# Moving the spline's scale from its absolute values to its clamps, with a planner that no longer holds engines back for the scan

## The chip, the cores and the metric

The kernel runs on one NeuronCore of a Trainium2 chip, as one launch. The metric is the device time in microseconds of one execution; lower is better. Short names of the engines: PE is TensorE (matmuls; PEld its weight loads), DVE is VectorE, ACT is ScalarE, POOL is GpSimd, SP is SyncE, which issues the DMAs here.

## The reference

The input `x` has shape (32, 128, 56, 56): 32 images, 128 channels, 3136 pixels each. Four residual layers follow each other, each `x = x + f(gn(x))`, where `gn` is a group normalisation over 32 groups of four channels:

- layer 0, dynamic convolution: a 128x128 mixing matrix made from the pooled image, then a depthwise 3x3 filter at three dilations, each through SiLU;
- layer 1, spline: each value is clipped to [-2, 2] and put through a cubic B-spline with ten coefficients and 14 knots;
- layer 2, linear attention: pooled 8x8 queries and keys, values from a 128x128 matrix, a depthwise 3x3 filter;
- layer 3, a Mamba layer: layer norm, projection, a causal filter of four taps, and a state-space scan.

The two parts that matter here, cut down:

```python
knots = jnp.linspace(GRID_MIN, GRID_MAX, NUM_KNOTS)      # -2, 2, 14
xc = jnp.clip(x, GRID_MIN, GRID_MAX)                     # x is group-normalised
basis = _bspline_basis(xc, knots)                        # cubic
return jnp.einsum('...n,n->...', basis, coeffs)
...
def step(h, inp):
    dA_t, dBu_t, C_t = inp
    h = dA_t * h + dBu_t                                 # 256 channels x 16 states
    y = jnp.einsum('bdn,bn->bd', h, C_t)
```

## The kernel before

**Tiles.** An image lives in SBUF as a tile of 128 channels by 3136 pixels (`xt`), worked on in seven chunks of 448 pixels. Three images are in flight: one in the scan, the next in layers 1 and 2, the one after that in layer 0. The hardware loop runs five times over six images; two images follow it, and a prologue prepares the first ones.

**The scan.** A chunk has 16 steps (`STEPS`), 112 per image. In each step:

- ACT makes the decays, two tiles `da <- delta,alog` of 128x448 in PSUM (`decay`). There are two such buffers in all, so a `da` waits until the scan of the step before has read its buffer.
- PE spreads the rows of B into `pb` once every two steps (`b_rows`, a single PSUM buffer), and of C into an `mm` tile, which ACT copies to `cb` (`c_rows`, two steps ahead).
- DVE multiplies `h <- du,pb` (128x896) and runs two scans `h <- da,last,h` (`state`). `h` has three buffers.
- ACT copies the last column to `last`, POOL multiplies `hc <- h,cb` (`products`; two buffers), and PE adds `hc` over the states into `y <- hc,sums` (`add`).

At a chunk's end DVE multiplies `sz` by `y`, PE applies `outT`, DVE adds to `xt`, and SP stores.

**The spline** (`spline`, from line 747). With u the normalised value in units of the knots' distance, it needs relu(1 - |u - m|) for the twelve inner knots m; linear combinations of these, two of them cubed, give the spline. For a chunk of 448 pixels SP copies 32 channels four times below each other (`stack <- xt`), so that four knots stand in one tile; three knot sets times four channel blocks make twelve `Abs` on ACT (128x448, line 801), and after every three a `Relu` over all three (128x1344, the clamp, line 803). A column operand of 128x1 gives each partition its own number: before, `Abs` takes both a scale `scl` and a bias `bia`, and the clamp only a bias `one`. `scl` and `bia` are made once per image: statistics (`group_stats`) give the mean `mg`, the variance with its epsilon `ve`, and `rs` = ve to the power -1/2; two columns `ab` are spread over the partitions by 16 small matmuls with `ident` into `pab`; DVE adds the knots' numbers `kneg` (line 517). `top` is the place above which the last basis function's end value is added.

**The order of the work.** All instructions outside the setup go through a planner (`Plan`). The calls only record pieces of work, each with its engine, the tiles it reads and writes, a price (`price`, line 163) and a step of the scan at which it stands. The planner derives due times backward through the dependencies, then goes forward in time (`attempt`, line 245): for each engine it picks among the pieces whose inputs are done, takes the one that can begin first over all engines, and so fixes the order in which each engine's in-order queue is written. Work of the scan and of the inputs of the next chunk is marked with `ahead > 0`; layers 0, 1 and 2 are filler with `ahead == 0`. Among one engine's pieces the choice is by

```python
late = at - self.PATIENCE[e] * (w.ahead > 0)
...
key = (max(late, free[e]), w.due, i)
```

Here `at` is when a piece can begin, and `free[e]` when its engine becomes free. A piece of the scan that will only be ready within `PATIENCE[e]` us of that is treated like one that is ready, and by its due time it usually goes first, with the engine idle until then. The planner's price for an activation adds 0.09 us for each column operand:

```python
columns = sum(isinstance(kw.get(k), bass.AP) for k in ("bias", "scale"))
w.cost += 0.06 + 8.34e-4 * n + 0.09 * columns + 0.03 * (args[1].space != bass.MemoryType.PSUM)
```

Since the planner's queues are issued from one place, nearly every instruction in the profile has the line of that place (L338); groups are told apart by the tiles' names.

Of the kernel before, what the change touches and what calls it, by code (L numbers as in the profile page):

```python
# [12 lines left out]
F32 = mybir.dt.float32  # L13
F32R = mybir.dt.float32r
AF = mybir.ActivationFunctionType
ALU = mybir.AluOpType
AX = mybir.AxisListType

P = 128
# [3 lines left out]
CH = ROWS * W  # L23
# [8 lines left out]
G = 32  # L32
NG = P // G
# [9 lines left out]
NKNOT = 14  # L43
GMIN, GMAX = -2.0, 2.0
# [49 lines left out]
class Plan:  # L94
# [7 lines left out]
    TABLE = 1.28  # L102
    NEVER = 1e18
    GATE, BUSY = 3.413, 1.27
    PATIENCE = {"tensor": 0.5, "scalar": 0.5, "gpsimd": 0.3, "vector": 0.1, "sync": 0.0}

    def __init__(self, nc, tc):
        self.nc, self.tc = nc, tc
# [136 lines left out]
    def attempt(self, born, behind):  # L245
# [6 lines left out]
        left = dict(self.uses)  # L252
        free = {e: 0.0 for e in self.PATIENCE}
        ready = {e: [] for e in self.PATIENCE}
        slots, held, table, bus, first, loads = {}, {}, None, 0.0, 0, {}
# [8 lines left out]
        while len(out) < len(works):  # L264
# [4 lines left out]
            for e, cand in ready.items():  # L269
                for i in cand:  # L270
# [6 lines left out]
                    if at >= self.NEVER:  # L277
                        continue
                    late = at - self.PATIENCE[e] * (w.ahead > 0)
                    if w.table and w.table != table:  # L280
# [82 lines left out]
def tile_conv_stack(ctx: ExitStack, tc: tile.TileContext, out: bass.AP, x: bass.AP, w: dict):  # L363
    nc = tc.nc
# [4 lines left out]
    def pool(name, bufs, **kw):  # L369
        return Rotation(plan, ctx.enter_context(tc.tile_pool(name=name, bufs=bufs, **kw)), name, bufs)  # L370

    const = ctx.enter_context(tc.tile_pool(name="const", bufs=1))
    small = pool("small", 2)
# [67 lines left out]
    def column(name, value):  # L441
        t = const.tile([P, 1], F32, name=name)
        nc.vector.memset(t[:], value)
        return t

    mhalf = column("mhalf", -0.5)
    one = column("one", 1.0)
# [62 lines left out]
    kneg = const.tile([P, len(KNOTS)], F32, name="kneg")  # L510
# [3 lines left out]
    for s, knots in enumerate(KNOTS):  # L514
        for k, m in enumerate(knots):
            rows = slice(G * k, G * k + G)
            nc.vector.memset(kneg[rows, s : s + 1], -float(m))
            for i, (f, s1) in enumerate(SUMS):
                if s1 == s and (f == 2 or m % 2 == f):
                    nc.vector.tensor_copy(cs[rows, i : i + 1], (qc if f == 2 else py_)[rows, m - 1 : m])  # L520
# [59 lines left out]
    nc = plan  # L580

    def psum(cols=CH, rows=P):
        t = ps_mm.tile([P, 512], F32, tag="mm", name="mm")
        return t[:rows, :cols]
# [15 lines left out]
    def group_stats(st):  # L600

        mv = small.tile([P, 2], F32, tag="mv", name="mv")
        nc.vector.bn_aggr(mv[:], st[:].rearrange("p a b -> p (a b)"))
        pm = psum(1)
        nc.tensor.matmul(pm, gmat[:], mv[:, 0:1], start=True, stop=True)
        mg = small.tile([P, 1], F32, tag="mg", name="mg")
        nc.vector.tensor_copy(mg[:], pm)
        dm = small.tile([P, 1], F32, tag="dm", name="dm")
        nc.vector.tensor_sub(dm[:], mv[:, 0:1], mg[:])
        vv = small.tile([P, 1], F32, tag="vv", name="vv")  # L610
        nc.vector.scalar_tensor_tensor(vv[:], dm[:], dm[:, 0:1], mv[:, 1:2], ALU.mult, ALU.add)
        pv = psum(1)
        nc.tensor.matmul(pv, gmat[:], vv[:], start=True, stop=True)
        ve = small.tile([P, 1], F32, tag="ve", name="ve")
        nc.vector.tensor_scalar_add(ve[:], pv, GN_EPS)
        rs = small.tile([P, 1], F32, tag="rs", name="rs")
        nc.gpsimd.tensor_tensor(rs[:], ve[:], mhalf[:], ALU.pow)
        return mg, rs, ve, dm
# [127 lines left out]

    def spline(xt, st):
        mg, rs, ve, _ = group_stats(st)
        ab = small.tile([P, 2], F32, tag="ab", name="ab")

        kpu = (NKNOT - 1) / (GMAX - GMIN)
        nc.vector.tensor_scalar_mul(ab[:, 0:1], rs[:], kpu)
        nc.vector.tensor_mul(ab[:, 1:2], mg[:], ab[:, 0:1])
        nc.vector.tensor_scalar(ab[:, 1:2], ab[:, 1:2], -1.0, -GMIN * kpu, ALU.mult, ALU.add)

        top = small.tile([P, 1], F32, tag="top", name="top")
        nc.vector.tensor_mul(top[:], ve[:], rs[:])
        nc.scalar.activation(top[:], top[:], AF.Identity, bias=mg[:, 0:1], scale=GMAX)
        pab = psum(2 * NG)
        for c in range(NG):  # L760
            for k in range(4):
                nc.tensor.matmul(
                    pab[G * k : G * k + G, 2 * c : 2 * c + 2],
                    ident[:, G * c : G * c + G],
                    ab[:],
                    start=True,
                    stop=True,
                    tile_position=(0, G * k),
                )
        pab = pab.rearrange("p (c t) -> p c t", t=2)  # L770
        scl = small.tile([P, NG], F32, tag="scl", name="scl")
        nc.vector.tensor_copy(scl[:].unsqueeze(2), pab[:, :, 0:1])
        bia = small.tile([P, NG, 3], F32, tag="bia", name="bia")
        nc.vector.tensor_add(
            bia[:], kneg[:].unsqueeze(1).to_broadcast([P, NG, 3]), pab[:, :, 1:2].to_broadcast([P, NG, 3])
        )

        def load_u(j):

            t = stk.tile([P, NG, ROWS * PW], F32, tag="stack", name="stack")  # L780
            with plan.together():
                for k in range(4):
                    for c in range(NG):
                        nc.sync.dma_start(
                            t[G * k : G * k + G, c, 0:CH], xt[G * c : G * c + G, j * CH : (j + 1) * CH]
                        )
            return t

        us = [load_u(0)]
        after = Stats(xt)  # L790
        yield 6.0
        for j in range(NCH):
            if j + 1 < NCH:
                us.append(load_u(j + 1))
            u = us[j]
            xs = xt[:, j * CH : (j + 1) * CH]
            hats = wide.tile([P, NG, 3, CH], F32, tag="wide", name="hats")
            for c in range(NG):
                for s in range(3):
                    nc.scalar.activation(  # L800
                        hats[:, c, s, :], u[:, c, 0:CH], AF.Abs, bias=bia[:, c, s : s + 1], scale=scl[:, c : c + 1]
                    )
                nc.scalar.activation(hats[:, c], hats[:, c], AF.Relu, bias=one[:, 0:1], scale=-1.0)
                yield 3.6
            ind = tmp.tile([P, CH], F32, tag="v", name="ind")
            nc.gpsimd.tensor_scalar(ind[:], xs, top[:, 0:1], clast, ALU.is_ge, ALU.mult)

            def combined(f):
                ps = psum()
                mine = [i for i, (f1, _) in enumerate(SUMS) if f1 == f]  # L810
                for i in mine:
                    with plan.together(NG):
                        for c in range(NG):
                            nc.tensor.matmul(
                                ps[G * c : G * c + G, :],
                                wspl[:, i, :],
                                hats[:, c, SUMS[i][1], :],
                                start=(i == mine[0]),
                                stop=(i == mine[-1]),
                                tile_position=(0, G * c),  # L820
                            )
                return ps

            ps = combined(2)
            nc.vector.tensor_add(xs, xs, ps)
            nc.gpsimd.tensor_add(xs, xs, ind[:])
            after.take(j)
            yield 2.2
            for f in range(2):
                ps = combined(f)  # L830
                sq = tmp.tile([P, CH], F32, tag="v", name="sq")
                nc.scalar.activation(sq[:], ps, AF.Square)
                cube = tmp.tile([P, CH], F32, tag="v", name="cube")
                nc.vector.tensor_mul(cube[:], sq[:], ps)
                nc.gpsimd.tensor_add(xs, xs, cube[:])
                yield 1.7
        after.take(NCH)
        return after.st
# [307 lines left out]
    def until_scan(b):  # L1146

        xt = xts[b % 3]
        st = yield from spline(xt, sts[b % 2])
        st = yield from linear_attention(xt, st)  # L1150
        norm = carried[b % 2]
        norm_weights(st, *norm)
        yield 5.0
        layer_norm(xt, xns[b * NCH % 3], 0, norm)
        yield 5.0
# [233 lines left out]
```

## Time and profile before

| what | us | from |
|---|---|---|
| median of three runs | 16343.33 (16294.26 to 16363.43) | the times |
| the profiled execution | 16316.11 | the times |
| its span in the profile | 16314.3 | the page |
| the scans `h<-da,last,h` and `h<-da,h` | 6772.7 + 1054.1, 7168 of them | groups of instructions |
| the products `h<-du,pb` | 3788.6, 3584 of them | groups of instructions |
| `hats<-stack,bia,scl` (the Abs) | 1887.6, 2688 of them at 754 ns | groups of instructions |
| `hats<-hats,one` (the clamps) | 1261.5, 896 of them at 1408 ns | groups of instructions |
| table loads of ACT | 656.9, 512 of them | groups of instructions |

A group's row gives the engine, the operation, the tiles written and read with their shapes, the count, the busy time and the mean duration of one, and then the time that the engine stood idle just before these instructions with what ended it. A row of the list of waits has the waiter, the one that released it, the total, the number of waits and the longest one. The busy times of engines overlap, so they don't add up to the span. PEclk is the granted clock of PE in tenths of full speed; it was 0.893 in the mean.

### The profile page before, as it was taken

Reading aid. Unit: us, or ns where it says so; the run is one execution under the profiler, and the core shown is the slowest. Engines: PE = TensorE matmul, PEld = TensorE weight load, DVE = VectorE, ACT = ScalarE, POOL = GpSimd, SP = SyncE. Lnnn points to the kernel's source line nnn. Section 1 sums busy time; section 2 is a strip of 40 time slices with the busy share of each in tenths; the row PEclk is TensorE's granted clock in tenths of the full one; section 3 lists DMA queues with packets and bytes.
Section 4 is the critical chain, followed back from the end, with each engine's and each line's share of the span. In section 5 each row is a group of like instructions: output and inputs, shape, how many; then the busy total and the mean of one; then the engine's idle time right before and its main releaser. Section 6 shows DMA issues by size and latency. Waiting matters only on the chain. (4 is left out here: it accounts for less than half of the span.)

```text
span 16314.3 us, 212520 instructions
## 1 busy us (share of the span) xinstructions
PE 14202.3 (87%) x66400; PEld 4559.9 (28%) x66400; DVE 14306.2 (88%) x17314; ACT 11713.4 (72%) x21127; POOL 10785.0 (66%) x6406
## 2 busy tenths in 40 slices
PE   6888898888898888988888888888888898888887
PEld 2222222222222222222222222222222222222222
DVE  2898988989889898899988888888898898888889
ACT  3777777777677776777776777767777677776675
POOL 2676666666666666667666666666676666766666
PEclk7888998889998898998989988899988899888888
DMA  6344444344443444434444434444344444344421
GB/s 143 93 101 98 98 112 96 89 99 101 106 104 88 100 97 101 109 94 94 101 99 107 102 86 98 99 105 107 91 98 97 100 108 106 85 97 99 101 56 34
DMA packets 986159, 1589.93 MB, mean 97 GB/s; under 512 B 175622, under 2 KB 611209, under 8 KB 984331
## 3 DMA queue, kind: packets, MB, share of 16 engines
q1 hardware_dynamic: 985002, 1576.06, 41.0%
q8 instruction: 538, 8.81, 0.2%
q14 instruction: 619, 5.06, 0.1%
HBM read 785.62 MB, written 173.18 MB: 59 GB/s over the span
## 5 line engine op out<-in xcount | busy, mean ns | idle before, releaser
L338 POOL TENSOR_TENSOR hc<-h,cb 128x896 f32<-128x896 f32 x3584 | 7476.1, 2092 | 4173.5 <-DVE h L338 2178.7
L338 DVE TENSOR_TENSOR_SCAN h<-da,last,h 128x448 f32<-128x448 f32 x6144 | 6772.7, 1135 | 498.2 <-ACT da L338 451.3
L338 ACT ACTIVATE da<-delta,alog 128x448 f32<-128x448 f32 x7168 | 4481.8, 633 | 2635.3 <-DVE h L338 2369.4
L338 PE MATMUL y<-hc,sums 128*64 128x448 f32 x14336 | 3997.9, 638 | 625.6 <-POOL hc L338 617.8
L338 DVE TENSOR_TENSOR h<-du,pb 128x896 f32<-128x896 f32 x3584 | 3788.6, 1072 | 247.5 <-POOL hc L338 118.2
L338 PE MATMUL mm<-stack,dsT 96*32 96x448 f32 (+1 forms) x16128 | 1890.8, 575 | 59.4 <-DMA stack<-padded 16.8
L338 ACT ACTIVATE hats<-stack,bia,scl 128x448 f32<-128x448 f32 x2688 | 1887.6, 754 | 33.9 <-DVE bia L338 31.7
L338 PE MATMUL mm<-xn,winT 128*128 128x448 f32 x3584 | 1703.8, 590 | 39.8 <-ACT cb L338 13.5
L338 PEld LDWEIGHTS y<-hc,sums 128*64 128x64 f32 x14336 | 807.6, 147 | 2412.9 <-POOL hc L338 1436.9
L338 PE MATMUL mm<-hats,wspl 128*32 128x448 f32 x12544 | 1386.1, 563 | 33.3 <-ACT hats L338 30.4
L338 PE MATMUL pb<-dbl,sel 64*128 64x448 f32 x1792 | 918.3, 512 | 421.2 <-DVE h L338 364.3
L338 ACT ACTIVATE hats<-hats,one 128x1344 f32<-128x1344 f32 x896 | 1261.5, 1408 | 0.1
L338 ACT COPY cb<-mm 128x448 f32<-128x448 f32 x1792 | 940.3, 527 | 379.4 <-POOL hc L338 184.0
L338 PE MATMUL mm<-dbl,sel 64*128 64x448 f32 x1792 | 892.3, 502 | 363.5 <-DVE sz L338 63.7
L338 ACT ACTIVATE t<-mm 128x448 f32<-128x448 f32 x1568 | 829.2, 534 | 484.6 <-PE mm L338 480.3
L338 POOL TENSOR_TENSOR xt<-xt,g 128x448 f32<-128x448 f32 x672 | 767.5, 1142 | 524.1 <-DVE g L338 491.1
L338 DVE TENSOR_TENSOR_SCAN h<-da,h 128x448 f32<-128x448 f32 x1024 | 1054.1, 1070 | 28.3 <-ACT da L338 26.3
L338 PEld LDWEIGHTS mm<-xn,winT 128*128 128x128 f32 x3584 | 631.8, 197 | 986.0 <-issue 805.1
L338 DVE SCALAR_TENSOR_TENSOR g<-t,mm 128x448 f32<-128x448 f32 x672 | 407.7, 607 | 443.7 <-ACT t L338 392.8
L338 PEld LDWEIGHTS mm<-stack,dsT 96*32 96x32 f32 (+1 forms) x16128 | 445.2, 112 | 1156.3 <-issue 899.9
L338 PEld LDWEIGHTS mm<-dbl,sel 64*128 64x128 f32 x1792 | 351.2, 198 | 1453.5 <-issue 420.0
L338 PEld LDWEIGHTS pb<-dbl,sel 64*128 64x128 f32 x1792 | 358.6, 200 | 1419.1 <-issue 791.8
(187 smaller groups left out, 16166.2 us busy)
## 6 DMA issues: line engine op xcount, KB each, us to landing
stack<-padded SPq DMA_DIRECT2D x2688, 264.0 KB
stack<-xt SPq DMA_DIRECT2D x3584, 56.0 KB
delta<-delta SPq DMA_DIRECT2D x1792, 112.0 KB
du<-du SPq DMA_DIRECT2D x1792, 112.0 KB
padded<-yc SPq DMA_DIRECT2D x224, 264.0 KB
padded<-yc SPq DMA_DIRECT2D x256, 231.0 KB
xt<-x_dram SPq DMA_DIRECT2D x224, 224.0 KB
out_dram<-xt SPq DMA_DIRECT2D x224, 224.0 KB
```

Of the source, the lines that this page charges most:

```text
L338: call()
```

## The change

It has two parts. The spline's `Abs` no longer scales: it takes |x - mean - knot x deviation| on the raw value, and the clamp multiplies by -kpu x rs and adds one. For that, `kneg` holds the negated knot in the spline's own units, `ab` has three columns (the negated scale, the deviation ve x rs, the negated mean), and `bia` is made by a multiplication and an addition. A chunk has twelve instructions with a column operand less and four with one more. Second, all of `PATIENCE` becomes zero, so the planner takes what can begin first and looks at due times only among pieces that could begin at the moment the engine is free. Both parts change the planner's inputs, so the order of nearly all queues is made anew.

```diff
-    PATIENCE = {"tensor": 0.5, "scalar": 0.5, "gpsimd": 0.3, "vector": 0.1, "sync": 0.0}
+    PATIENCE = {"tensor": 0, "scalar": 0, "gpsimd": 0, "vector": 0, "sync": 0.0}
...
-            nc.vector.memset(kneg[rows, s : s + 1], -float(m))
+            nc.vector.memset(kneg[rows, s : s + 1], -GMIN - m * (GMAX - GMIN) / (NKNOT - 1))
...
-        ab = small.tile([P, 2], F32, tag="ab", name="ab")
+        ab = small.tile([P, 3], F32, tag="ab", name="ab")
         kpu = (NKNOT - 1) / (GMAX - GMIN)
-        nc.vector.tensor_scalar_mul(ab[:, 0:1], rs[:], kpu)
-        nc.vector.tensor_mul(ab[:, 1:2], mg[:], ab[:, 0:1])
-        nc.vector.tensor_scalar(ab[:, 1:2], ab[:, 1:2], -1.0, -GMIN * kpu, ALU.mult, ALU.add)
+        nc.vector.tensor_scalar_mul(ab[:, 0:1], rs[:], -kpu)
+        nc.vector.tensor_mul(ab[:, 1:2], ve[:], rs[:])
+        nc.vector.tensor_scalar_mul(ab[:, 2:3], mg[:], -1.0)
...
-        nc.vector.tensor_mul(top[:], ve[:], rs[:])
-        nc.scalar.activation(top[:], top[:], AF.Identity, bias=mg[:, 0:1], scale=GMAX)
-        pab = psum(2 * NG)
+        nc.scalar.activation(top[:], ab[:, 1:2], AF.Identity, bias=mg[:, 0:1], scale=GMAX)
+        pab = psum(3 * NG)
...
-        nc.vector.tensor_add(
+        nc.vector.tensor_mul(
             bia[:], kneg[:].unsqueeze(1).to_broadcast([P, NG, 3]), pab[:, :, 1:2].to_broadcast([P, NG, 3])
         )
+        nc.vector.tensor_add(bia[:], bia[:], pab[:, :, 2:3].to_broadcast([P, NG, 3]))
...
-                        hats[:, c, s, :], u[:, c, 0:CH], AF.Abs, bias=bia[:, c, s : s + 1], scale=scl[:, c : c + 1]
+                        hats[:, c, s, :], u[:, c, 0:CH], AF.Abs, bias=bia[:, c, s : s + 1]
                     )
-                nc.scalar.activation(hats[:, c], hats[:, c], AF.Relu, bias=one[:, 0:1], scale=-1.0)
+                nc.scalar.activation(hats[:, c], hats[:, c], AF.Relu, bias=one[:, 0:1], scale=scl[:, c : c + 1])
```

The matmuls that spread `ab` change their column ranges from two to three per block in the same way.

More of the change, by code (lines that the diff above doesn't have):

```diff
@@ L762, in spline @@
                 nc.tensor.matmul(
-                    pab[G * k : G * k + G, 2 * c : 2 * c + 2],
+                    pab[G * k : G * k + G, 3 * c : 3 * c + 3],
                     ident[:, G * c : G * c + G],
@@ L769, in spline @@
                 )
-        pab = pab.rearrange("p (c t) -> p c t", t=2)
+        pab = pab.rearrange("p (c t) -> p c t", t=3)
         scl = small.tile([P, NG], F32, tag="scl", name="scl")
```

## The prediction

> **What bounds the kernel now.** I read the page's head first (busy shares and slices), then the groups of instructions with shapes kept apart, then the list of waits cut to the steady stretch from 1000 to 15000 us, and last a few microseconds of the timeline.
>
> ```profile
> span 16314.3 us, 212520 instructions
> PE 14202.3 (87%) x66400; PEld 4559.9 (28%) x66400; DVE 14306.2 (88%) x17314; ACT 11713.4 (72%) x21127; POOL 10785.0 (66%) x6406
> PE   6888898888898888988888888888888898888887
> DVE  2898988989889898899988888888898898888889
> PEclk7888998889998898998989988899988899888888
> 1000.00:15000.00 14000.00, 12336.88 (x58154) 3956.94 (x58153) 12502.68 (x15049) 10237.22 (x18488) 9440.08 (x5604) 0.90 0.42 99
> ```
>
> The last row, busy time in the steady stretch, is ordered PE, weight load, DVE, ACT, POOL, clock, DMA share, GB/s. No engine is full: VectorE works 12503 of 14000 us (89%) and TensorE 12337 (88%) at a clock of 0.90. VectorE carries the scan and sets the pace, TensorE is right behind it, and the 14000 - 12503 = 1497 us of VectorE idle are what a different order can win; work taken from ScalarE (73%) pays only through them. Who causes them (waiter <- releaser: total us, times, longest):
>
> ```profile
> ACT da L338 <- DVE h L338: 2085.4, 2515, 3.8
> PE y L338 <- POOL hc L338: 521.7, 609, 2.8
> DVE h L338 <- ACT da L338: 421.7, 438, 3.0
> PE pb L338 <- DVE h L338: 313.2, 314, 4.2
> DVE g L338 <- ACT t L338: 258.8, 159, 5.3
> DVE h L338 <- POOL hc L338: 104.0, 79, 3.0
> DVE h L338 <- PE pb L338: 79.7, 104, 1.9
> ```
>
> ScalarE stands still before da for 2085 us because the two PSUM tiles of da are held by the scan: that is patience, and free. TensorE stands still before y and pb for 835 us: that is patience on an engine nearly full. The largest single loss of VectorE is a decay that comes late, 422 us in 438 waits, mean 0.96 us. One such place (start, us, engine, op; idle before it in brackets):
>
> ```profile
> 3047.88 1.40 ACT L338 ACTIVATE hats<-stack,bia,scl 128x448 f32<-128x448 f32 x2
> 3049.18 0.62 ACT L338 ACTIVATE yc<-mm,aggb 128x448 f32<-128x448 f32 x1
> 3049.70 1.40 ACT L338 ACTIVATE hats<-hats,one 128x1344 f32<-128x1344 f32 x1
> 3051.00 1.18 ACT L338 ACTIVATE da<-delta,alog 128x448 f32<-128x448 f32 x2
> 3051.66 4.35 DVE L338 TENSOR_TENSOR_SCAN h<-da,last,h 128x448 f32<-128x448 f32 x4 [3.02 <-ACT da L338]
> ```
>
> Spline work stood ahead of da on ScalarE's in-order queue and VectorE lost 3.02 us. The change makes such work shorter, and at the same time lets it go first more often.
>
> **What the Trainium skill says.** "ScalarE: Activation LUTs", What ACT_TABLE_LOAD costs: each [128,1] pointer operand of an ACTIVATE adds about 93 ns. The trace agrees: sq<-mm takes 532 ns without and 628 ns with a bias column (96), du<-du 949 and 1034 (85). "TensorE: Matmul & The Clock Gate", HAM oscillation: the clock drops when TensorE idles for about a window, so a fuller TensorE stays fast; the trace shows 0.90 in the steady stretch and 0.77 in the first 450 us, where TensorE is busy for 298. "Perfetto Trace Analysis", Optimizing Scalar/DVE Operations: an engine that isn't full can still make bubbles on others, and shorter instructions then help. The timeline above is such a bubble.
>
> **The change part by part.**
> 1. Twelve Abs of a chunk lose the scale column. Row: hats<-stack,bia,scl x2688 at 754 ns. With 92 ns less each: 2688 x 0.092 = -247 us of ScalarE. The four clamps gain one: hats<-hats,one x896 at 1408 ns, + 896 x 0.09 = +81 us. Net -166 us of 11713 (1.4%). This lies mostly beside VectorE's work. To see what reaches VectorE I compared, for the six images of the loop body and in the old order, the ScalarE work between two da with the VectorE work between the two scans, at the trace's durations, and let a lead of one scan (1.1 us) carry over. The excess of ScalarE falls by 6% with the shorter hats (319 to 300 us; used as a share only). 6% of the page's 478 us of VectorE idle behind da (451.3 + 26.3) is -30 us. Bounds: 0 if they always have cover, -166 if each saving lies on the path. I take -30.
> 2. The setup of the spline, once per image: top and ab's second column become one product, bia takes a multiply and an add, the transposing matmuls carry three columns for two. VectorE loses one 0.33 us row (top<-ve,rs) and gains one of 0.15 (like bia<-kneg,mm): about -6 us over 32 images. The slow ab product (1.05 us mean) stays as another product in the same place. 16 matmuls of 0.19 us with one column more: nothing. The chain before the first hats keeps its length. Taken as 0; within +-30.
> 3. Patience 0. It touches no instruction, only the order, on all queues: the planner, with lower prices for Abs and no allowance, orders everything anew (ScalarE's queue goes from 4219 to 4369 rows of equal neighbours, TensorE's from 3590 to 3628, POOL's 995 to 1026, SP's 1022 to 1008). The number of table loads doesn't change. Three effects:
>  a. ScalarE. With the loop taken five times, 4678 of 7168 da stood behind other work and 5034 do so now (+356): Abs ahead of da grows from 577 to 777, clamps 636 to 650. Behind a waiting da stand its scan, then hc and y. The same comparison as in 1, in the new order with the new durations, gives 317 for 300 us, +6%, or +28 us. Bounds: 0, and 356 x 0.96 us = +342 if each added filler makes its da late by the mean of today's late ones.
>  b. TensorE. It no longer stands before y (618 us on the page) and pb (364) while ready matmuls wait. If I cut both orders into scan steps and add the larger of TensorE's and VectorE's work in each step, at the trace's durations, the excess over VectorE alone falls from 700 to 620 us for six images; over two steps from 496 to 458 (-8%); over eight from 190 to 186. So the new order is more even where it counts, over a few steps. 8% of the 1497 us of idle: -120 us. Bounds: -490 if half of the 982 us of TensorE's waits is won; +180 if pb, which has a single buffer and stands before the next product h, is 0.5 us later in each of its 360 waits (a matmul pair takes 1.02 us in the timeline).
>  c. POOL, SP, VectorE. hc stands behind other POOL work in 342 places of the program for 317; POOL is 66% busy, h has three buffers and VectorE waits 118 us for hc on the whole page. SP's order changes, with transfers at 42% of the queues' share and 21 us of VectorE idle before h behind du's transfer. Cover stays; 0, or +60 if hc's wait grows by half.
>
> Sum: -30 + 0 + 28 - 120 + 0 = -122 us against the profiled execution's 16316, or 16194. That execution is 27 us under the median of the three runs (16343), which would give 16221; I say **16205 us**, 0.8% below the median. Late next: the same three waits, each smaller, with VectorE at about 89%.
>
> **Rivals.**
> - *Slower: late decays.* Place: ScalarE's queue in the stretches where hats run. A clamp is now about 1.50 us and no longer gives way to a da that becomes ready within 0.5 us. Between the release of a da tile and its use lie one scan and one product of VectorE (1.1 + 1.07) less the da itself (0.6): some 1.5 us. A clamp with any small operation behind it exceeds this. Price: +342 (3a's bound) - 30 - 40 (a third of 3b) = +272, or 16615; from some 180 late da more than now (x 0.96 = 172, against the 150 of 1 and 3b) it decides the sign. For: 356 more da with filler ahead. Against: in the new order the very long stretches are fewer (138 gaps of over 4 us between da fall to 96, in the program as written).
> - *No change.* VectorE's own 14306 us stay, and what one wait frees another takes; TensorE's gain disappears since eight-step stretches hardly differ (190 and 186). About 16340.
> - *TensorE's clock rises.* If filling its gaps lifts the clock from 0.90 to 0.92, as in some stretches of the trace, TensorE's 14202 us shrink by 2%, 284 us, and half of that, since VectorE limits too, joins the rest: 16060.
> - *The change does not do what it says*: the order could have stayed. It hasn't, as the row counts show.
>
> **How the numbers follow.** Chances: forecast 0.42, clock 0.10, no change 0.16, late decays 0.32. About 0.5% (80 us) is what a measurement of this kernel can tell from none. Faster 0.52, same 0.16, slower 0.32. The forecast's own range, from the bounds of 1 and 3b against 3a, is 16020 to 16290. The whole range takes in the clock case and most of the late decays, whose typical case I set at half of its bound: 15960 to 16560.
>
> **What would show it.** hats<-stack at about 660 ns and the clamp at about 1500, ScalarE's busy time some 166 us lower: step 1. TensorE's waits y <- hc and pb <- h down from 618 and 364, TensorE's share up: step 3b. VectorE's wait for da near 478 us: 3a small. If it exceeds 650 us, the slower rival is right; if h <- pb grows well over 89 us, TensorE's fillers delay pb. The forecast is wrong if VectorE's share doesn't rise above 88%.

## The result

The changed kernel took 16066.35 us (median of 4 runs, 16031.57 to 16080.3) where the kernel before took 16351.42 us beside it: a ratio of 0.983, 95% interval 0.9805 to 0.9855. It is faster by 1.7%, about twice the forecast's 0.8%.

The head of the page after and its row of busy time in the stretch from 1000 to 15000 us (PE, weight load, DVE, ACT, POOL, then clock, DMA share and GB/s):

```profile
span 16029.6 us, 213040 instructions
PE 14120.8 (88%) x66400; PEld 4536.4 (28%) x66400; DVE 14308.5 (89%) x17314; ACT 11542.0 (72%) x21127; POOL 10781.3 (67%) x6406
1000.00:15000.00 14000.00, 12488.22 (x59243) 4011.98 (x59240) 12739.84 (x15319) 10300.39 (x18875) 9619.78 (x5714) 0.90 0.43 101
```

VectorE's work is what it was (14306.2 us before, 14308.5 after), so the 285 us between the spans are idle time of VectorE that is gone. TensorE's clock didn't rise in this stretch (0.90 in both), and over the whole span it went from 0.893 to 0.896, not to the 0.92 at which the prediction priced that rival. The groups with shapes kept apart (count | busy us, mean ns | idle us just before, by releaser) show the two new forms of the hats (`Abs` and clamps together), and where the idle time went. Before:

```profile
L338 DVE TENSOR_TENSOR_SCAN h<-da,last,h 128x448 f32<-128x448 f32 x6144 | 6772.7, 1135 | 498.2 <-ACT da L338 451.3
L338 DVE TENSOR_TENSOR h<-du,pb 128x896 f32<-128x896 f32 x3584 | 3788.6, 1072 | 247.5 <-POOL hc L338 118.2 <-PE pb L338 88.7 <-DMA du<-du 20.8
```

After:

```profile
L338 ACT ACTIVATE hats<-stack,bia 128x448 f32<-128x448 f32 x2688 | 1658.9, 666 | 2.8 <-issue 1.9 <-DVE bia L338 0.9
L338 ACT ACTIVATE hats<-hats,one,scl 128x1344 f32<-128x1344 f32 x896 | 1346.6, 1503 | 1.1
L338 DVE TENSOR_TENSOR_SCAN h<-da,last,h 128x448 f32<-128x448 f32 x6144 | 6757.0, 1134 | 336.1 <-ACT da L338 294.7
L338 DVE TENSOR_TENSOR_SCAN h<-da,h 128x448 f32<-128x448 f32 x1024 | 1063.3, 1072 | 20.4 <-ACT da L338 20.2
L338 DVE TENSOR_TENSOR h<-du,pb 128x896 f32<-128x896 f32 x3584 | 3783.7, 1071 | 185.5 <-PE pb L338 74.7 <-POOL hc L338 64.6 <-DMA du<-du 17.1
L338 DVE TENSOR_TENSOR sz<-sz,y 128x448 f32<-128x448 f32 x448 | 270.4, 608 | 189.9 <-PE y L338 189.9
```

Before, VectorE stood 478 us ahead of the scans for a decay da (451.3 + 26.3); now it is 315. That is 163 of the 285 us. The product h<-du,pb gives 62 more (247.5 to 185.5); a part comes back at sz<-sz,y (99.2 to 189.9) and at ws<-mm,rs (15.6 to 88.5), both behind TensorE. The rest of the 285 us is spread over many groups, 57 us the largest of them. The list of waits of the whole run has what the prediction's step on TensorE spoke of, and the wait for da. Before, then after:

```profile
PE y L338 <- POOL hc L338: 617.8, 697, 6.3
PE pb L338 <- DVE h L338: 364.3, 360, 15.8
DVE h L338 <- ACT da L338: 478.9, 503, 3.0
```

```profile
PE y L338 <- POOL hc L338: 703.7, 469, 14.1
PE pb L338 <- DVE h L338: 249.0, 313, 15.8
DVE h L338 <- ACT da L338: 320.7, 434, 10.9
```

Of TensorE's two waits, one fell and the other rose; their sum went from 982 to 953 us. So the question for the experiments: two edits were made together, one of durations, one of order, and both reorder everything. Which of them is it, and through what?

### The profile page after: what moved, and what is told of

Its sections match the earlier page's. It is cut to its first block, busy times and chain, and to the rows that moved or that the text cites. A ratio compares the mean times of both kernels' runs of the same rounds, so it can differ in the third digit from the quotient of the medians.

```text
span 16029.6 us, 213040 instructions
## 1 busy us (share of the span) xinstructions
PE 14120.8 (88%) x66400; PEld 4536.4 (28%) x66400; DVE 14308.5 (89%) x17314; ACT 11542.0 (72%) x21127; POOL 10781.3 (67%) x6406
## 5 line engine op out<-in xcount | busy, mean ns | idle before, releaser
L338 PE MATMUL y<-hc,sums 128*64 128x448 f32 x14336 | 3961.8, 631 | 705.2 <-POOL hc L338 703.7
L338 DVE TENSOR_TENSOR h<-du,pb 128x896 f32<-128x896 f32 x3584 | 3783.7, 1071 | 185.5 <-PE pb L338 74.7
L338 ACT ACTIVATE hats<-stack,bia 128x448 f32<-128x448 f32 x2688 | 1658.9, 666 | 2.8 <-issue 1.9
L338 PE MATMUL mm<-hats,wspl 128*32 128x448 f32 x12544 | 1457.9, 577 | 64.8 <-ACT hats L338 34.0
L338 ACT ACTIVATE hats<-hats,one,scl 128x1344 f32<-128x1344 f32 x896 | 1346.6, 1503 | 1.1
L338 PE MATMUL pb<-dbl,sel 64*128 64x448 f32 x1792 | 907.0, 506 | 275.7 <-DVE h L338 249.0
L338 PE MATMUL mm<-xn,wzT 128*128 128x448 f32 x896 | 612.1, 775 | 143.3 <-DVE cube L338 65.9
L338 POOL TENSOR_TENSOR xt<-xt,cube 128x448 f32<-128x448 f32 x448 | 511.9, 1143 | 326.1 <-DVE cube L338 320.3
```

The source lines that it names most:

```text
L338: call()
```

## The experiments

Each result is a median beside runs of the kernel before on the same chip; the ratio is to those, with its 95% interval.

### One part at a time

*patience_only*: the old spline, PATIENCE all zero.

```diff
-    PATIENCE = {"tensor": 0.5, "scalar": 0.5, "gpsimd": 0.3, "vector": 0.1, "sync": 0.0}
+    PATIENCE = {"tensor": 0, "scalar": 0, "gpsimd": 0, "vector": 0, "sync": 0.0}
```

> The old spline with all of PATIENCE at zero. Theory A (the order: engines no longer stand idle for scan work that is not ready) expects most of the gain here: 0.985 to 0.990 of the time before, about 16110 to 16190 us. Theory B (the shorter absolute values) expects 0.995 to 1.010. Theory C (any new order lands somewhere within a per cent or so, by chance) gives no side.

Measured: 16494.41 us, 1.0084 (1.0067 to 1.0101). Slower.

*spline_only*: the new spline as in the change (its setup too, not shown here), PATIENCE as before.

```diff
-                        hats[:, c, s, :], u[:, c, 0:CH], AF.Abs, bias=bia[:, c, s : s + 1], scale=scl[:, c : c + 1]
+                        hats[:, c, s, :], u[:, c, 0:CH], AF.Abs, bias=bia[:, c, s : s + 1]
...
-                nc.scalar.activation(hats[:, c], hats[:, c], AF.Relu, bias=one[:, 0:1], scale=-1.0)
+                nc.scalar.activation(hats[:, c], hats[:, c], AF.Relu, bias=one[:, 0:1], scale=scl[:, c : c + 1])
```

> The new spline with the old PATIENCE. Theory A expects little: 0.996 to 1.000 (16290 to 16350 us), since ScalarE is 72% busy and the shorter hats mostly lie beside VectorE's work. Theory B expects 0.985 to 0.990, with VectorE's wait for da down from 479 us to about 320 us as after the whole change.

Measured: 16573.29 us, 1.0138 (1.0121 to 1.0155). Slower as well. Each half alone loses, and both together win 1.7%: theories A and B fall in their simple form.

### The same order with other durations

Two kernels hold an order fixed and change only how long the hats take. The planner is told the price that goes with that order, so no queue moves.

*old_order*: the old kernel's queues, the new columns. The Abs works on the raw value here, so this spline isn't the reference's.

```diff
             columns = sum(isinstance(kw.get(k), bass.AP) for k in ("bias", "scale"))
+            if method == "activation" and args[2] == AF.Abs and n == CH and args[1].space != bass.MemoryType.PSUM:
+                columns = 2
+            if method == "activation" and n == 3 * CH:
+                columns = 1
...
-        nc.vector.tensor_scalar_mul(ab[:, 0:1], rs[:], kpu)
+        nc.vector.tensor_scalar_mul(ab[:, 0:1], rs[:], -kpu)
...
-        nc.vector.tensor_scalar(ab[:, 1:2], ab[:, 1:2], -1.0, -GMIN * kpu, ALU.mult, ALU.add)
+        nc.vector.tensor_scalar(ab[:, 1:2], ab[:, 1:2], 1.0, -GMIN * kpu, ALU.mult, ALU.add)
...
-    AF.Abs, bias=bia[:, c, s : s + 1], scale=scl[:, c : c + 1]
+    AF.Abs, bias=bia[:, c, s : s + 1]
...
-    AF.Relu, bias=one[:, 0:1], scale=-1.0)
+    AF.Relu, bias=one[:, 0:1], scale=scl[:, c : c + 1])
```

> Exactly the order of before on every queue, with the shorter hats: Abs has only the bias column and the clamp has the scale column, and the planner is told the old prices so that nothing moves. Abs takes the raw value instead of the scaled one, so the spline's values are not the reference's; no instruction is left out. Theory A expects 0.997 to 0.999: the 166 us of ScalarE reach the end with 20 to 50 us. If the savings lie on the path (theory B) it is 0.990 (the whole 166 us).

Measured: 16303.88 us, 0.9971 (0.996 to 0.9982): 42 us reach the end (29 to 65 by the interval), of 166 by count; the page shows ScalarE 138 us less busy (11575.7).

*two_columns*: the changed kernel's queues, with a second column for each Abs; the planner's lines are those of old_order with 1 and 2 for 2 and 1.

```diff
-                        hats[:, c, s, :], u[:, c, 0:CH], AF.Abs, bias=bia[:, c, s : s + 1]
+                        hats[:, c, s, :], u[:, c, 0:CH], AF.Abs, bias=bia[:, c, s : s + 1], scale=one[:, 0:1]
```

> Exactly the order of the changed kernel on every queue, with a second column given back to each Abs (a scale of one), so ScalarE is 247 us busier than in the changed kernel and 81 us busier than before. Theory A expects the gain to stay: 0.983 to 0.989 of before, 16080 to 16170 us. Theory B expects that 0.990 or more is left, since the saving is gone.

Measured: 16155.14 us, 0.9876 (0.9859 to 0.9894). With ScalarE 81 us busier than before by count, a gain of 1.2% stays. It is the order, which both parts made, that gives it; the shorter Abs give the rest of the 1.7%, some 0.4 to 0.5%. The wait for da, in old_order and then in two_columns, each from its own list:

```profile
DVE h L342 <- ACT da L342: 446.2, 412, 3.1
```

```profile
DVE h L342 <- ACT da L342: 399.3, 533, 12.0
```

So of the way from 478.9 us before to 320.7 after, the new order takes 80 us and the shorter Abs within it the other 79.

### Why the patience alone was slower: a table that holds the hats

In the trace of patience_only I looked for VectorE's long pauses. In each image of the loop there is one of 12.5 us in the second chunk of the scan, and in one image of six another of 10.2 us in the third. The timeline around one of them (start, us, engine, op; idle before in brackets), ScalarE's hats and the waiting scan:

```profile
4591.89 1.28 ACT L338 ACT_TABLE_LOAD   x1
4593.18 0.63 ACT L338 ACTIVATE rstd<-mm,lneps 128x448 f32<-128x448 f32 x1
...
4594.65 0.75 ACT L338 ACTIVATE hats<-stack,bia,scl 128x448 f32<-128x448 f32 x1
...
4595.73 1.40 ACT L338 ACTIVATE hats<-stack,bia,scl 128x448 f32<-128x448 f32 x2
...
4597.55 1.40 ACT L338 ACTIVATE hats<-hats,one 128x1344 f32<-128x1344 f32 x1
...
4599.87 2.08 ACT L338 ACTIVATE hats<-stack,bia,scl 128x448 f32<-128x448 f32 x3
...
4602.36 1.42 ACT L338 ACTIVATE hats<-hats,one 128x1344 f32<-128x1344 f32 x1
...
4604.08 2.74 ACT L338 ACTIVATE hats<-stack,bia,scl 128x448 f32<-128x448 f32 x4
...
4606.69 1.43 ACT L338 ACTIVATE hats<-hats,one 128x1344 f32<-128x1344 f32 x1
...
4608.00 1.42 ACT L338 ACTIVATE hats<-stack,bia,scl 128x448 f32<-128x448 f32 x2
4609.45 1.41 ACT L338 ACTIVATE hats<-hats,one 128x1344 f32<-128x1344 f32 x1
...
4610.87 1.28 ACT L338 ACT_TABLE_LOAD   x1
...
4612.65 1.18 ACT L338 ACTIVATE da<-delta,alog 128x448 f32<-128x448 f32 x2
...
4613.30 2.19 DVE L338 TENSOR_TENSOR_SCAN h<-da,last,h 128x448 f32<-128x448 f32 x2 [12.55 <-ACT da L338]
```

Between two table loads (logarithm in, exponential back) all sixteen hats of a chunk run, 19 us, with every da behind them. The reason lies in the planner's rule: exponentials count as 0.6 us later while the other table is loaded (`late += 0.6`), hats need no table, and the choice is by the later of that and the engine's free time, before any due time. So every hat that is ready goes before the table is switched back. A patience of 0.5 doesn't outweigh the 0.6. Counted over the traces, windows of this kind with hats in them were 0 before, 36 in patience_only (of some 255 in each kernel), 20 in spline_only (with fifteen hats each) and 1 in the changed kernel; VectorE's idle time in all windows, from one load to about a microsecond past the next, was some 273, 772, 527 and 284 us.

*patience_gate, spline_gate, after_gate*: a rule that lets hats wait while that table is loaded, put into patience_only, spline_only and the changed kernel. Put into the kernel before, it leaves every queue as it was.

```diff
                         late += 0.6
+                    if table == "ln" and not w.table and w.writes[0] and "hats" in w.writes[0][0]:
+                        late += 0.7
```

> The old spline with PATIENCE zero, and one rule more in the planner: while ScalarE's logarithm table is loaded, hats wait (they count as 0.7 us later). Theory D: patience_only was slow because in 35 of its 254 logarithm windows the planner let a whole chunk's hats run before it switched the table back, with the da behind them; VectorE's idle in these windows was 772 us against 273 before. It expects those 500 us back: 15980 to 16080 us, 0.978 to 0.984. Theory C (an order is good or bad by chance, the windows don't matter) expects 0.995 to 1.01.

Measured: 16311.45 us, 0.9972 (0.9963 to 0.9982).

> The new spline with the old PATIENCE and the same rule for hats. Its 20 windows with hats had 527 us of VectorE's idle in all windows, 254 more than before. Theory D expects 16290 to 16350 us, 0.996 to 1.000: the old order's time with the small gain of the shorter hats. Theory C expects it to stay at 1.005 to 1.014.

Measured: 16485.51 us, 1.0076 (1.0057 to 1.0095).

> The changed kernel with the rule for hats. It had one window with hats in the whole run (10.9 us of idle), so Theory D expects the changed kernel's time or up to 15 us less: 0.981 to 0.984 of before. Theory C expects up to half a per cent either way, since the order moves after that window.

Measured: 16083.94 us, 0.9839 (0.982 to 0.9857), the changed kernel's time within the intervals.

Removing the windows with hats won back less than half of what they had shown: 183 us of the 500 expected in one kernel and 88 of 254 in the other. VectorE's idle time in the windows did fall, to some 299 and 365 us in all, but most of the gain was lost elsewhere in the new order. Their waits for da (and after_gate's for pb) afterward, in this order patience_gate, spline_gate, after_gate (each from its own list of waits):

```profile
DVE h L340 <- ACT da L340: 443.4, 468, 2.5
```

```profile
DVE h L340 <- ACT da L340: 532.4, 553, 3.3
```

```profile
DVE h L340 <- ACT da L340: 316.6, 445, 2.4
DVE h L340 <- PE pb L340: 79.0, 98, 2.3
```

So theory D explains why patience alone was slower than before; it doesn't explain most of the new spline's loss under the old patience (1.0138 to 1.0076), nor why both parts together are faster.

### Luck of the order, or the two parts together

*after_jitter, before_jitter, patience_jitter, spline_jitter*: the four corners with the rule for hats, and one price of the planner moved by 10 ns, which says nothing about the chip and makes another order.

```diff
-    HOP = {"tensor": 0.24, "vector": 0.17, "scalar": 0.13, "gpsimd": 0.1, "sync": 0.2}
+    HOP = {"tensor": 0.24, "vector": 0.18, "scalar": 0.13, "gpsimd": 0.1, "sync": 0.2}
```

> The same as after_gate with the planner's hop from VectorE priced at 0.18 us for 0.17: nothing but another order of the same kind, to see how far an order alone moves the time. Theory D expects 0.980 to 0.988 (the gain belongs to the kind of order), theory C 0.985 to 1.005.

Measured: 16144.45 us, 0.9876 (0.9857 to 0.9894).

> The kernel before with the rule for hats (which alone leaves its order as it is) and VectorE's hop priced at 0.18 us for 0.17. Theory C (an order's luck) expects anything from 0.995 to 1.012, and says that the order of before was one draw of many; Theory E (the two parts of the change work only together) expects 0.997 to 1.003.

Measured: 16251.77 us, 0.995 (0.9934 to 0.9967).

> patience_gate with the same other hop. Theory C expects some 0.4% either way of patience_gate's 0.997, so 0.990 to 1.004, and if the draw falls near 0.988 the interaction seen so far is luck. Theory E expects 0.994 to 1.000.

Measured: 16202.69 us, 0.9923 (0.9907 to 0.994).

> spline_gate with the same other hop. Theory C expects 0.998 to 1.012 around spline_gate's 1.008, and a mean over draws at about 0.997 of the old spline's orders; Theory E expects 1.004 to 1.012.

Measured: 16533.04 us, 1.0117 (1.01 to 1.0134).

Two draws (orders) for each corner, ratio to the kernel before; the first entry, 1.000, is that kernel itself:

| | old PATIENCE | PATIENCE zero |
|---|---|---|
| old spline | 1.000, 0.995 | 0.9972, 0.9923 |
| new spline | 1.0076, 1.0117 | 0.9839, 0.9876 |

A meaningless price moves the time by 0.4 to 0.5% in every corner, so an order's luck is real and of the size of the smaller effects here. But the pattern holds in both draws: by the means, patience zero wins 0.3% with the old spline and 2.4% with the new one; the new spline loses 1.2% under the old patience and wins 0.9% under zero. If the two parts simply added up, both together would stand at 1.0048 in the first draw (1.0076 + 0.9972 - 1.000) and at 1.009 in the second; they stand 2.1% lower in each. Neither theory was right alone: C's scatter and E's interaction are both there. Two draws are few, but the interaction is some four times what the moved price did to any corner.

### TensorE's patience

*tensor_patience*: after_gate with TensorE's 0.5 put back.

```diff
-    PATIENCE = {"tensor": 0, "scalar": 0, "gpsimd": 0, "vector": 0, "sync": 0.0}
+    PATIENCE = {"tensor": 0.5, "scalar": 0, "gpsimd": 0, "vector": 0, "sync": 0.0}
```

> after_gate with TensorE's patience back at 0.5 us, the other engines' at zero. If the gain came from TensorE no longer standing idle for the scan (step 3b of the prediction), it is gone: 0.995 to 1.005, with TensorE's waits for hc and for h up. If ScalarE's order gives it, 0.980 to 0.990 stays. If it is luck of the order, anything between.

Measured: 16157.49 us, 0.9894 (0.9877 to 0.991). Its list of waits:

```profile
PE y L340 <- POOL hc L340: 596.5, 582, 4.6
PE pb L340 <- DVE h L340: 302.2, 434, 15.9
DVE h L340 <- POOL hc L340: 140.4, 150, 1.6
DVE h L340 <- ACT da L340: 381.7, 447, 4.3
DVE h L340 <- PE pb L340: 26.1, 45, 1.6
```

Of after_gate's gain of 1.6%, 1.1% stays. Putting TensorE's patience back costs 73 us by the medians and some 90 us by the ratios, little above what the moved price did to this corner (60 us), so with one draw it can't be told from an order's luck. The waits don't bear out step 3b: TensorE's two waits add up to 899 us with patience and 949 without (hc 597 and 696, pb 302 and 253). VectorE waits less for pb with it (26 against 79) and before sz for y (85 against 210), but more for da (382 against 317) and for hc (140 against 63). As far as one draw tells, most of the gain then lies with the patience of ScalarE, POOL or VectorE; these were not tried one by one, and which of them it is, and why it needs the new spline, stays open.

### What goes with the time

Over all kernels without windows of hats, the sum of VectorE's two waits inside the scan, for da and for pb, follows the time from group to group:

| kernel | da + pb, us | time, us |
|---|---|---|
| after_gate | 396 | 16084 |
| tensor_patience | 408 | 16157 |
| after_jitter | 422 | 16144 |
| patience_jitter | 537 | 16203 |
| patience_gate | 540 | 16311 |
| old_order | 543 | 16304 |
| before_jitter | 553 | 16252 |
| before | 568 | 16343 |
| spline_gate | 706 | 16486 |
| spline_jitter | 722 | 16533 |

From the first to the last row 326 us more of these waits go with 449 us more of time. Within the middle group, 537 to 568 us, they don't order the times (16203 to 16343 us). This is a correlation, not an experiment; but it points to the scan's own inputs as the place where good and bad orders of this kernel differ.

A rival was not tested: the granted clock of TensorE moved with the order as well. It was 0.893 in the profile of before and 0.894 in after_gate, but 0.885 in patience_gate and 0.884 in spline_gate. Over 32 executions of the kernel before, with clocks of 0.890 to 0.896, a clock lower by 0.001 goes with about 9 us more (a line fitted to the times on record). By that, an estimate, the lower clock stands for 70 to 80 us in each of those two corners, and without it the interaction would be about 1.2% in the first draw and 1.6% in the second instead of 2.1%. The clock doesn't order the kernels by itself: patience_gate at 0.885 was faster than before at 0.893, and tensor_patience at 0.897 slower than after_gate at 0.894. Nor did a fuller TensorE have the higher clock: it was busy for 88% of the span in patience_gate and 87% before. Whether it is a cause of these times or only goes with them stays open.

## Why the prediction was right, and where it was wrong

The direction and the range were right; the sum of -122 us was less than half of what came (-285). VectorE's share did rise, to 89%, as the forecast asked. Two of the steps behind the number don't hold, so part of its being right is luck.

1. Shorter hats. The durations were right: 666 ns and 1503 ns, ScalarE 171 us less busy (11713.4 to 11542.0) for 166 predicted. The term for what reaches the end, -30, was about right in the old order: old_order measured -42 us (29 to 65), 33 of them in the wait for da (478.9 to 446.2). In the new order more arrives: between two_columns and the changed kernel, or after_gate, which has the same order up to its one window, some 60 to 90 us of the 247 us of the Abs. So a quarter to a third of ScalarE's saving reaches the end, where the sum took 18%.
2. The setup was taken as 0. Its VectorE rows took 14 us more (56.6 to 70.6) where 6 us less were forecast, since the slow ab product went from 1046 to 1656 ns; in patience_only, with the old spline, it took 1589 ns, so this goes with the order. ScalarE stood 50.9 us before top for 7.3. No run prices the setup alone.
3. a. ScalarE's order was put at +28 us of late decays. The wait for da fell by 158 us on the list of waits instead, and the 80 us of it that two_columns still shows are the order's. That a da has other work ahead of it more often (+356) didn't make it late; the count says nothing of whether the da could have started. The sign of this term was wrong.
 b. TensorE was to give -120 us by no longer standing before y and pb, the largest term of the sum. It read these waits as patience. Without patience they were 953 us (703.7 + 249.0) for 982, and 942 (712.3 + 229.6) in patience_gate, so patience was not the main thing that held TensorE there. tensor_patience leaves 73 to 90 us to TensorE's patience, near the size of the term, but not through these waits and hardly clear of an order's luck. The tally of evenness pointed the right way, by luck as far as its reason goes.
 c. POOL: VectorE's wait for hc fell from 118 to 65 us rather than staying or growing.

What the prediction had not seen at all: the two parts aren't additive. It priced them one after another and added, and alone both are losses (1.0084 and 1.0138).

The rival of late decays came true, but in patience_only: VectorE's wait for da went from 479 to 668 us there. Its mechanism was one clamp in the way of one da; what the trace shows is a whole chunk of hats behind a table switch, 12.5 us at a time. The changed kernel escapes it in all but one window. Why its hats aren't ready in those windows was not tried.

The Trainium skill's price of about 93 ns for a column operand ("ScalarE: Activation LUTs", What ACT_TABLE_LOAD costs) held in both directions: 88 ns less for each Abs (754 to 666) and 95 more for each clamp (1408 to 1503).

## What to carry to other kernels

Where a planner writes the order, an edit of prices or preferences is a new order, and two such edits aren't priced separately; run each corner, and run each again with a meaningless price moved, to see how much an order's luck is worth (0.4 to 0.5% here). To price a duration by itself, hold the order fixed by telling the planner the old price. When work without a table is let ahead of a table switch, look between the table loads for whole backlogs that pass there. And when two orders are compared, note the granted clock of each beside its time.

## What the runs showed that was not expected

A quarter to a third of a saving on ScalarE reached the end although that engine stood idle for 28% of the span. A price of 10 ns in the planner, with the same instructions, made the kernel before 0.5% faster. And the switch of ScalarE's table cost 1.29 us from its start to the start of the next activation (4591.89 to 4593.18 in the timeline above), the load's own 1.28 us and no more (over all loads in the trace of the kernel before the median is 1.295 us); what made it dear in patience_only was the work let through between two of them.
